# A two-layer graph kernel on one core: upper slot layers cut to a tile's last nodes, and a start-up written out in order

## The chip, the core and the metric

One core of one Trainium2 chip runs the whole program. The metric is device time in microseconds, from launch to end. The engines are PE (matmul, with its weight loads shown as PEld), DVE (vector), ACT (scalar), POOL (GpSimd, which also issues the indirect transfers) and SP (which only issues transfers). DMA transfers are issued by SP, ACT and POOL and are carried out by the core's 16 DMA engines.

## The reference, cut to what matters

There are 4096 nodes with 128 features each and a 0/1 adjacency matrix of 4096 x 4096 with about 32 neighbours a node. Two layers follow each other.

```python
# layer 0: graph attention, 8 heads
Wh = einsum('nd,hde->hne', nodes, W)
e = leaky_relu(f1[:, :, None] + f2[:, None, :], 0.2)      # f1 = Wh.a1, f2 = Wh.a2
att = softmax(where(adj > 0, e, -9e15), axis=-1)
h = elu(einsum('hnm,hmd->hnd', att, Wh))
x = layernorm(nodes + elu(concat_heads(h) @ W1 + b1)) * gamma + beta
# layer 1: neighbours, less every m-th one, sorted per feature; three quantiles
keep = mask & ~((rank + 1) % skip == 0)
svals = sort(where(keep, x, big), axis=1)
agg = mean of svals at ceil(q * n_keep) - 1, q in (0.25, 0.5, 0.75)
out = (0.5 * agg + 0.5 * x) @ W.T + b + x
```

## The kernel before, in words

The kernel works with lists of neighbours instead of the matrix. It has these stages.

**Search.** `neighbours` reads 128 rows of adj in two halves of 1 MB (`adj_t`, issued by ACT), turns each into signs on ACT (`sgn`, which also counts), and lets PE add, in PSUM tiles `key` of 512 columns, the sign times 8192 and a falling number of the column (`parts`, filled by POOL; `markb` and `oneb` are the fixed operands). DVE takes the eight largest of every 128 columns (`first`, L592) and then, in eight rounds, the largest 64 of those (L597 and L599). A tile of 128 nodes is eight such pieces; the selection runs one tile behind. `complete_records` works out, per group of up to four tiles, which neighbours layer 1 drops.

**Blocks.** The 32 tiles are taken in three blocks of 4, 9 and 19 (`BLOCKS`). Inside a block `rank_by_count` sorts the nodes by their number of neighbours (`ranks`), and POOL scatters their records (`rec`, list, own number, features, f1, f2) to DRAM in that order, so that each tile of a block then holds nodes of like count. `CAPS` gives the most neighbours that a node of each sorted tile may have.

**Attention for a tile.** `read_lists` loads the 128 records (`R`, four loads by SP) and spreads the lists into layers: a layer `(s0, w)` covers the list places from s0 to s0 + w of all 128 nodes with w gathers, each of which serves P // w nodes (`k`) completely. A layer narrower than 32 needs its own four loads by SP (`narrow`) and its own small DVE operations; there is one `narrow` buffer for each width. `fetch_rows` issues one indirect gather (L194, POOL) for each slot, 128 rows of 544 bytes from `xt_d` (features and f2) into tiles `G` of 16 slots, of which there are six. `attend` adds f1 (`z`), applies the exponential, sums it per node on PE (`den`, own) and hands the sum back (`rz`, ownT), with P // w // 4 matmuls for each layer in each of the two; it then spreads the weights (`wide`, L932) and multiplies every slot's rows on PE (`y`, L944). The dense part and the layer norm follow, and POOL scatters the 128 finished rows to `x1_d`.

**Order.** In the blocks the order on DVE, PE, ACT and POOL is the order of the code (`manual_schedule`). Each `step` issues the gathers of one tile, attends the tile before it, prepares the lists two tiles ahead and mixes in a share of the search of the next block. In the last tile of a block, the rest of the search and `rank_by_count` come first on DVE, and the scatters of the next block's records are mixed into that tile's gathers on POOL, one after every two, beginning when so few gathers are left that they just suffice:

```python
if among and left % 2 == 0 and left <= 2 * len(among) + 4:
    scatter(nc, *among.pop(0))
```

The next block's first lists can be loaded only after the last of these scatters has landed.

**Start.** Before the first block the constants (`own`, `ownT` and others) are made, the search of block 0 runs (L317), and `node_rows` loads W, x, a1 and a2, forms `wa`, transposes the 32 tiles of x on PE one at a time, multiplies them by `wa` to get f1 and f2 (`F`) and stores features and f2 to `xt_d`. Here the framework's scheduler chooses the order on the engines; x, W and a1, a2 are loaded by SP.

**Layer 1.** After the 32 tiles, 1024 gathers fetch the rows of `x1_d`, and DVE runs a sorting network cut to what the quantiles need (L1155). If any count exceeds its bound (`bad`, summed into `total`), a general path behind L501 computes everything again.

Of the kernel before, what the change touches and what calls it, by code (L numbers as in the profile page):

```python
# [9 lines left out]
F32 = mybir.dt.float32  # L10
# [44 lines left out]

TURNS = {4: range(4), 9: range(9), 19: [0, 1, 2, 3, 18, 4, 5, 6, 7, *range(9, 18), 8]}
# [33 lines left out]
def layers(c):  # L90


    out = []
    s = 0
    for w in (32, 32, 16, 8, 4):
        if (c + 3) // 4 * 4 - s >= w:
            out.append((s, w))
            s += w
    return out

# [117 lines left out]
def kernel(  # L218
# [33 lines left out]
    iota(nc, pidx, [[0, 1]], cm=1)  # L252
    jp1 = const.tile([P, L], F32, name="jp1")
    iota(nc, jp1, [[1, L]], base=1)

    own = {}
    for w in (32, 16, 8, 4):
        k = P // w
        v = const.tile([P, k], F32, name=f"v{w}")
        iota(nc, v, [[-w, k]], cm=1)  # L260
        own[w] = const.tile([P, k], F32, name=f"own{w}")
        nc.vector.tensor_scalar(own[w], v, 0.0, None, ALU.is_ge)
        nc.vector.scalar_tensor_tensor(own[w], v, float(w), own[w], ALU.is_lt, ALU.mult)


    ownT = {}
    for w in (32, 16, 8, 4):
        k = P // w // 4
        v = const.tile([4, k, P], F32, name=f"vT{w}")
        iota(nc, v, [[-4 * w, k], [1, P]], cm=-w)  # L270
        ownT[w] = const.tile([4, k, P], F32, name=f"ownT{w}")
        nc.vector.tensor_scalar(ownT[w], v, 0.0, None, ALU.is_ge)
        nc.vector.scalar_tensor_tensor(ownT[w], v, float(w), ownT[w], ALU.is_lt, ALU.mult)

# [3 lines left out]
    nc.sync.dma_start(W_sb, W.rearrange("h d e -> d h e"))  # L278
# [4 lines left out]
    consts = dict(  # L283
        W_sb=W_sb, W1_sb=W1_sb, vecs=vecs, eps_t=eps_t, ident=ident, own=own, ownT=ownT
    )
# [11 lines left out]
    nc.gpsimd.iota(  # L297
        rec.bitcast(I32)[:, :, R_OWN], pattern=[[P, NT]], base=0, channel_multiplier=1
    )
    parts = adjp.tile([64, N], BF16, name="parts", bufs=1)  # L300
    markb = adjp.tile([P, P], BF16, name="markb", bufs=1)
    nc.vector.memset(oneb, 1.0)
    nc.vector.tensor_scalar(markb, ident, MARK, None, ALU.mult)

    nc.gpsimd.memset(parts, 0.0)
    iota(nc, parts[0:1, :], [[-64, N // 64], [0, 64]], base=N)
    iota(nc, parts[32:33, :], [[0, N // 64], [-1, 64]])
    rowi = adjp.tile([P, P], F32, name="rowi", bufs=1)
    iota(nc, rowi, [[1, P]])
    nc.vector.tensor_scalar(before, rowi, pidx, None, ALU.is_gt)  # L310
# [6 lines left out]
    for _ in search(0, BLOCKS[0]):  # L317
        pass
    with tc.tile_pool(name="setup", bufs=1) as sp, tc.tile_pool(
        name="setup_ps", bufs=2, space=PSUM  # L320
    ) as pp:
        node_rows(tc, sp, pp, rec, x, W_sb, a1, a2, Wl, wa, WlT, ident, bad, xt_d)
# [3 lines left out]
        for i, big in enumerate((-BIG, BIG)):  # L326
            fill = sp.tile([P, D], F32, name=f"fill{i}")
            nc.vector.memset(fill, big)
            nc.sync.dma_start(x1_d[N + i * P : N + (i + 1) * P, :], fill)
# [6 lines left out]
    weigh, store, tail = [], [], []  # L336
    consts["small"] = pp.tile([P, 512], F32, name="small")
# [6 lines left out]

    def prepare(b, i, t0):
        n = BLOCKS[b]
        i = TURNS[n][i]
        return read_lists(tc, attp, recs_d[b], i, CAPS[n][i], t0 + i, bad, narrow)
# [49 lines left out]
    with tc.manual_schedule(engines=ORDERED):  # L398
        ranks = rank_by_count(tc, cp, kp, num, jp1, before, oneb, 0, BLOCKS[0])
        for v in store_records(0, 0, ranks):  # L400
            scatter(nc, *v)
        for b, n in enumerate(BLOCKS):
# [103 lines left out]
def node_rows(tc, sp, pp, rec, x, W_sb, a1, a2, Wl, wa, WlT, ident, bad, xt_d):  # L506

    nc = tc.nc
    c = NT // 4
    for i in range(4):  # L510
        nc.sync.dma_start(
# [3 lines left out]
    a_b = sp.tile([P, 2, H * D], F32, name="a_b")  # L515
    for i, a in enumerate((a1, a2)):
        nc.sync.dma_start(a_b[:, i, :], a.rearrange("h d -> (h d)").partition_broadcast(P))
    wl_sb = sp.tile([P, D], F32, name="wl_sb")
    nc.scalar.dma_start(wl_sb, Wl)
    wl_ps = pp.tile([P, D], F32, name="xt_ps")  # L520
    nc.tensor.transpose(wl_ps, wl_sb, ident)
    nc.scalar.copy(WlT, wl_ps)
    for i in range(2):
# [4 lines left out]
        nc.vector.tensor_reduce(wa[:, ts(i, H)], wprod, AX.X, ALU.add)  # L528
    F = sp.tile([P, NT, 2 * H], F32, name="F")
    for t in range(NT):  # L530
        xt_ps = pp.tile([P, P], F32, name="xt_ps")
        nc.tensor.transpose(xt_ps, rec[:, t, R_X : R_X + D], ident)
        xT = sp.tile([P, P], F32, name="xT", bufs=2)
        nc.scalar.copy(xT, xt_ps)
        f_ps = pp.tile([P, 2 * H], F32, name="f_ps")
        nc.tensor.matmul(f_ps, lhsT=xT, rhs=wa, start=True, stop=True)
        nc.scalar.copy(F[:, t, :], f_ps)
    for dst, src in ((R_F1, F[:, :, 0:H]), (R_X + D, F[:, :, H:])):
        nc.vector.tensor_scalar(rec[:, :, dst : dst + H], src, FMAX, -FMAX, ALU.min, ALU.max)
    sq = sp.tile([P, NT, 2 * H], F32, name="sq")  # L540
# [6 lines left out]
    for i in range(4):  # L547
        nc.sync.dma_start(
            xt_d[ts(i, c * P), :].rearrange("(t p) w -> p t w", p=P),
            rec[:, ts(i, c), R_X:],  # L550
        )
    pad = sp.tile([P, XW], F32, name="pad")
    nc.vector.memset(pad[:, 0:D], 0.0)
    nc.vector.memset(pad[:, D:], PADF)
# [873 lines left out]
```

## Time and profile before

| what | value |
|---|---|
| median of 3 runs | 4632.38 us (4607.63 to 4632.42) |
| profiled execution, its own time | 3702.95 us |
| its span | 3701.2 us |
| PE, DVE, ACT, POOL busy | 1228.3, 2746.5, 403.4, 2421.0 us |
| gathers of `G` (L194) | 1180, 1174.8 us busy, mean 996 ns, 478.8 us idle before them |
| gathers of `vals` (layer 1) | 1024, 1052.1 us busy |
| mean granted TensorE clock | 0.581 |

The profile is of one execution, which was shorter than the timed runs. Busy time is what an engine's instructions took; the idle time of a group is what its engine waited just before the group's instructions, with the releaser that ended most of it. A line such as L194 is that of a helper and gathers all its callers; the tile names tell them apart.

### The profile page before, as it was taken

What the parts mean: (1) busy time and instruction counts of PE and PEld (TensorE: products, weight loads), DVE (VectorE), ACT (ScalarE), POOL (GpSimd) and SP (SyncE); (2) the same over time, 40 slices, a digit from 0 to 9 for tenths busy, and PEclk for the clock granted to TensorE, in tenths of its full rate; (3) what the DMA queues carried; (4) which work ended last, traced back from release to release, by engine and by line L of the source; (5) the groups of instructions that cost most, each with busy time, mean ns of one, the idle gap of its engine ahead of it and who ended that gap; (6) DMA issues with size and microseconds to landing.
All of it is one profiled execution on the core that took longest, in us unless ns stands there. A gap on an engine that the chain in (4) does not pass through costs nothing. (4 is left out here: it accounts for less than half of the span.)

```text
span 3701.2 us, 23191 instructions
## 1 busy us (share of the span) xinstructions
PE 1228.3 (33%) x5433; PEld 936.3 (25%) x5433; DVE 2746.5 (74%) x7565; ACT 403.4 (11%) x603; POOL 2421.0 (65%) x2388
## 2 busy tenths in 40 slices
PE   6483767773673544454450000000000000000011
PEld 2043544453562443444440000000000000000011
DVE  8774688782541222127637999999999999999998
ACT  3121222220120111111110000000000000000000
POOL 1657674467777777777747777677657565667630
PEclk9975676655575555565555555555555555555555
DMA  6432544322222221222211111111111111111100
GB/s 211 156 99 67 182 137 136 128 72 62 59 54 55 53 55 52 53 66 57 55 33 49 47 47 46 43 46 46 37 38 48 36 42 40 44 44 49 42 19 3
DMA packets 110291, 241.33 MB, mean 65 GB/s; under 512 B 46976, under 2 KB 63360, under 8 KB 101952
## 3 DMA queue, kind: packets, MB, share of 16 engines
q0 software_dynamic: 76160, 160.24, 15.5%
q10 hardware_dynamic: 9360, 67.18, 5.2%
q1 hardware_dynamic: 24624, 12.34, 1.4%
q8 instruction: 45, 0.74, 0.1%
q14 instruction: 102, 0.84, 0.1%
HBM read 228.44 MB, written 11.15 MB: 65 GB/s over the span
## 5 line engine op out<-in xcount | busy, mean ns | idle before, releaser
L194 POOL DMA_INDIRECT G<-xt_d,idx x1180 | 1174.8, 996 | 478.8 <-issue 336.4
L194 POOL DMA_INDIRECT vals<-x_d,idx x1024 | 1052.1, 1027 | 337.6 <-issue 298.5
L1155 DVE TENSOR_TENSOR work<-work 128x512 f32<-128x512 f32 (+6 forms) x1405 | 961.0, 714 | 0.4
L1174 PE MATMUL st_ps<-dg,goal 128*128 128x128 f32 x286 | 71.2, 426 | 1645.3 <-DVE goal L1155 1574.9
L1155 DVE TENSOR_TENSOR work<-work,work 128x512 f32<-128x512 f32 (+5 forms) x958 | 606.4, 658 | 0.7
L1174 PEld LDWEIGHTS st_ps<-dg,goal 128*128 128x128 f32 x286 | 63.2, 322 | 1651.7 <-issue 1650.8
L944 PE MATMUL y<-wide,G 128*128 128x32 f32 (+3 forms) x2360 | 460.3, 371 | 23.9 <-DVE wide L932 23.9
L944 PEld LDWEIGHTS y<-wide,G 128*128 128x128 f32 x2360 | 440.2, 286 | 47.5 <-DVE wide L932 26.3
L887 DVE TENSOR_TENSOR z<-G,f1x 128x128 f32<-128x128 f32 (+2 forms) x92 | 29.9, 335 | 471.5 <-DMA G<-xt_d,idx 467.3
L592 DVE MAX8 first<-key 128x8 f32<-128x128 f32 x1024 | 227.8, 282 | 108.4 <-PE key L628 108.3
L203 POOL DMA_INDIRECT out_dram<-o,own_i x32 | 45.6, 1425 | 297.4 <-ACT o L1200 277.8
L625 PE MATMUL key<-sgn,markb 128*128 128x512 bf16 x256 | 141.6, 554 | 162.3 <-DVE first L592 108.9
L1126 DVE COPY junk<-still 128x1 f32<-128x1 f32 x1295 | 194.7, 150 | 0.0
L901 PE MATMUL small<-z,own 128*4 128x32 f32 (+3 forms) x436 | 50.2, 284 | 380.6 <-ACT z L894 380.6
L1155 DVE TENSOR_TENSOR work<-vals 128x1024 f32<-128x1024 f32 (+8 forms) x140 | 138.8, 1009 | 46.4 <-DMA vals<-x_d,idx 46.1
L586 ACT ACTIVATE sgn<-adj_t 128x2048 bf16<-128x2048 int32 x64 | 122.0, 1907 | 340.7 <-PE key L625 304.5
L1173 ACT ACTIVATE dg<-ident,wt 128x128 f32<-128x128 f32 x143 | 47.5, 394 | 957.2 <-PE st_ps L1174 956.8
L916 PE MATMUL rz<-rden,ownT 4*128 4x32 f32 (+3 forms) x436 | 104.7, 411 | 117.3 <-DVE rden L912 96.0
L628 PE MATMUL key<-parts,oneb 64*128 64x512 bf16 x256 | 140.4, 549 | 6.3 <-POOL parts L212 6.3
L974 PE MATMUL small<-W_sb,late 128*128 128x128 f32 x512 | 118.7, 425 | 33.5 <-DVE late L971 33.5
L901 PEld LDWEIGHTS small<-z,own 128*4 128x4 f32 x436 | 27.1, 102 | 398.1 <-ACT z L894 385.8
L916 PEld LDWEIGHTS rz<-rden,ownT 4*128 4x128 f32 x436 | 91.9, 302 | 133.5 <-DVE rden L912 68.4
(179 smaller groups left out, 1891.7 us busy)
## 6 DMA issues: line engine op xcount, KB each, us to landing
adj_t<-in_adj_dram ACTq DMA_DIRECT2D x64, 1024.0 KB
G<-xt_d,idx POOLq DMA_INDIRECT x1180
vals<-x_d,idx POOLq DMA_INDIRECT x1024
R<-rec_d SPq DMA_DIRECT2D x128, 26.2 KB
xt_d<-rec SPq DMA_DIRECT2D x4, 544.0 KB
rec<-in_x_dram SPq DMA_DIRECT2D x4, 512.0 KB
W_sb<-in_L_gnn_W_dram SPq DMA_DIRECT2D x2, 512.0 KB
a_b<-in_L_gnn_a_dram SPq DMA_DIRECT2D x2, 512.0 KB
```

Of the source, the lines that this page charges most:

```text
L194: nc.gpsimd.indirect_dma_start(out=dst, out_offset=None, in_=rows, in_offset=bass.IndirectOffsetOnAxis(ap=idx, axis=0),)
L586: nc.scalar.activation(sgn, adj_t, AF.Sign, accum_out=cnt[:, i : i + 1])
L592: nc.vector.max(first[:, ts(c0 // CW + c, 8)], key[:, ts(c, CW)])
L625: nc.tensor.matmul(key, lhsT=markb, rhs=sgn[:, ts(b, 512)], start=True, stop=False)
L628: nc.tensor.matmul(key, lhsT=oneb[0:64, :], rhs=parts[:, ts(r, 512)], start=False, stop=True)
L901: nc.tensor.matmul(den[0:4, :].rearrange("p (g r h) -> p r g h", r=k // 4, h=H)[:, r], lhsT=own[w][:, ts(r, 4)], rhs=z[:, layer[i] : layer ...
L916: nc.tensor.matmul(rz[:, layer[i] * H : (layer[i] + w) * H], lhsT=ownT[w][:, r, :], rhs=rden.rearrange("p (g r h) -> p r g h", r=k // 4, h ...
L944: nc.tensor.matmul(yf[:, ts(g, c)], lhsT=G[:, col + g - g0, 0:D], rhs=pf[:, ts(g, c)], start=(i == 0 and g % (w // 2) == w // 2 - 1), stop ...
L974: nc.tensor.matmul(o, lhsT=hv[:, h, :], rhs=consts["W1_sb"][:, h, :], start=(h == 0), stop=(h == H - 1))
L1126: nc.vector.tensor_copy(junk, late["still"])
L1155: nc.vector.tensor_tensor(slots_of(dst, (j, c, s, m), size), slots_of(a, (i, c, s, m), size), slots_of(b, (i + d, c, s, m), size), op,)
L1174: nc.tensor.matmul(st_ps[:, u, :], lhsT=goal[:, (j * k + u) * D : (j * k + u + 1) * D], rhs=dg, start=(j == 0), stop=False,)
```

## The change

The change has two parts. First, a layer may begin at a node group other than the first: `(s0, w, g0)` leaves out the gathers below g0, so that only the last nodes of the sorted tile get these places. `LAYERS` lists such layers for eleven tiles; elsewhere the layers are as before. The bound on the counts then rises along the tile (`steps_of`, `nodeq`).

```diff
+LAYERS = {
+    (4, 1): [(0, 32, 0), (32, 8, 7)],
+    (4, 2): [(0, 32, 0), (32, 4, 0), (36, 8, 7)],
+    (4, 3): [(0, 32, 0), (32, 16, 0), (48, 16, 15)],
+    (9, 0): [(0, 16, 0), (16, 8, 0), (24, 4, 2)],
+    (9, 4): [(0, 32, 0), (32, 4, 1)],
+    (9, 6): [(0, 32, 0), (32, 4, 0), (36, 4, 2)],
+    (9, 8): [(0, 32, 0), (32, 16, 0), (48, 16, 14)],
+    (19, 1): [(0, 16, 0), (16, 8, 0), (24, 4, 1)],
+    (19, 9): [(0, 32, 0), (32, 4, 2)],
+    (19, 17): [(0, 32, 0), (32, 8, 0), (40, 4, 1)],
+    (19, 18): [(0, 32, 0), (32, 16, 0), (48, 16, 13)],
+}
+def steps_of(parts):
+    held = [0] * P
+    for s0, w, g0 in parts:
+        for q in range(g0 * P // w, P):
+            if held[q] == s0:
+                held[q] += w
+    return held[0], [(q, held[q] - held[q - 1]) for q in range(1, P) if held[q] > held[q - 1]]
...
 def read_lists(...)
-    nc.vector.tensor_scalar(bad[:, 4, t : t + 1], R[:, R_NUM : R_NUM + 1], float(cap), None, ALU.is_gt)
+    cap, rises = min(cap, steps_of(layer_list)[0]), steps_of(layer_list)[1]
+    over = R[:, R_NUM : R_NUM + 1]
+    for q, more in rises:
+        up = ap.tile([P, 1], F32, name="up", bufs=3)
+        nc.vector.tensor_scalar(up, nodeq, float(q), -float(more), ALU.is_ge, ALU.mult)
+        nc.vector.tensor_tensor(up, up, over, ALU.add)
+        over = up
+    nc.vector.tensor_scalar(bad[:, 4, t : t + 1], over, float(cap), None, ALU.is_gt)
...
 def fetch_rows(...)
-        for g in range(w):
+        for g in range(g0, w):
...
 def attend(...)      # z, den, rz, wide and y work on w - g0 slots of a layer
-                rhs=z[:, layer[i] : layer[i] + w, :],
+                rhs=z[:, layer[i] : layer[i] + w - g0, :],
...
-        spread = [P, w, k, H]
+        spread = [P, n, k, H]          # n = w - g0
```

Second, everything up to the first gather is put under `manual_schedule`. The number rows are split in two tiles of 512 and 3584 columns, cleared on DVE; `own` and `ownT` are made after the scatters of block 0; the loads of W, a1, a2, Wl and x are issued by ACT; and `node_rows` becomes a generator that is advanced once after each search piece of block 0, with rows of x transposed four tiles at a time.

```diff
-    nc.gpsimd.memset(parts, 0.0)
-    iota(nc, parts[0:1, :], [[-64, N // 64], [0, 64]], base=N)
-    iota(nc, parts[32:33, :], [[0, N // 64], [-1, 64]])
-    for _ in search(0, BLOCKS[0]):
-        pass
...
+    ) as pp, tc.manual_schedule(engines=ORDERED):
+        for v in parts:
+            nc.vector.memset(v, 0.0)
+        nc.vector.memset(oneb, 1.0)
+        for v, base in zip(parts, (N, N - N // 8)):
+            n = v.shape[1] // 64
+            iota(nc, v[0:1, :], [[-64, n], [0, 64]], base=base)
+            iota(nc, v[32:33, :], [[0, n], [-1, 64]])
+        nc.vector.tensor_scalar(markb, ident, MARK, None, ALU.mult)
+        iota(nc, pidx, [[0, 1]], cm=1)
...
+        rows = node_rows(tc, sp, pp, rec, x, W, W_sb, a1, a2, Wl, wa, WlT, ident, bad, xt_d)
+        for i, _ in enumerate(search(0, BLOCKS[0])):
+            if i > 0:
+                next(rows, None)
+        for _ in rows:
+            pass
+        nc.vector.tensor_scalar(before, rowi, pidx, None, ALU.is_gt)
...
         for v in store_records(0, 0, ranks):
             scatter(nc, *v)
+        own = {}            # own and ownT, as they were, now here
...
 def node_rows(...)
+    load = nc.scalar.dma_start
+    load(W_sb, W.rearrange("h d e -> d h e"))
+    yield
+    for i, a in enumerate((a1, a2)):
+        load(a_b[:, i, :], a.rearrange("h d -> (h d)").partition_broadcast(P))
+    load(wl_sb, Wl)
+    yield
     for i in range(4):
-        nc.sync.dma_start(
+        for _ in range(3):
+            yield
+        load(
             rec[:, ts(i, c), R_X : R_X + D],
             x[ts(i, c * P), :].rearrange("(t p) d -> p t d", p=P),
         )
...
-    for t in range(NT):
-        xt_ps = pp.tile([P, P], F32, name="xt_ps")
-        nc.tensor.transpose(xt_ps, rec[:, t, R_X : R_X + D], ident)
-        xT = sp.tile([P, P], F32, name="xT", bufs=2)
-        nc.scalar.copy(xT, xt_ps)
-        f_ps = pp.tile([P, 2 * H], F32, name="f_ps")
-        nc.tensor.matmul(f_ps, lhsT=xT, rhs=wa, start=True, stop=True)
-        nc.scalar.copy(F[:, t, :], f_ps)
+    for t in range(0, NT + 8, 4):
+        if f_ps is not None:
+            nc.scalar.copy(F[:, t - 8 : t - 4, :], f_ps)
+            f_ps = None
+        if xT is not None:
+            f_ps = pp.tile([P, 4, 2 * H], F32, name="f_ps")
+            for u in range(4):
+                nc.tensor.matmul(f_ps[:, u, :], lhsT=xT[:, ts(u, P)], rhs=wa, start=True, stop=True)
+            xT = None
+        yield
+        if t < NT:
+            xt_ps = pp.tile([P, 4 * P], F32, name="xt_ps")
+            for u in range(4):
+                nc.tensor.transpose(xt_ps[:, ts(u, P)], rec[:, t + u, R_X : R_X + D], ident)
+            xT = sp.tile([P, 4 * P], F32, name="xT", bufs=2)
+            nc.scalar.copy(xT, xt_ps)
+        yield
```

## The prediction

> **What bounds the kernel now.** I read the page first: one core, span 3701.2 us, DVE 74% busy, POOL 65%, no engine full. The chain view is of no use here (it names only the last 32 us), so I went to busy time by stage, then to the timelines of POOL and DVE at the seams between stages.
>
> ```profile
> 270.00:358.00 88.00, 43.29 (x189) 35.22 (x189) 42.09 (x146) 9.59 (x9) 67.13 (x67) 0.56 0.21 58
> 358.00:843.00 485.00, 345.26 (x1429) 221.82 (x1429) 384.21 (x1468) 127.14 (x132) 300.00 (x305) 0.64 0.41 129
> 843.00:1884.00 1041.00, 522.79 (x2694) 479.19 (x2693) 369.34 (x1114) 129.22 (x142) 795.15 (x790) 0.58 0.22 56
> ...
> 1924.00:3701.00 1777.00, 125.56 (x542) 107.35 (x542) 1723.82 (x3944) 57.33 (x180) 1130.83 (x1087) 0.52 0.14 40
> ```
> Columns: stretch, its length, busy PE, PEld, DVE, ACT, POOL with instruction counts, clock, DMA share, GB/s. From 270 to 358 and from 843 to 1884 POOL sets the pace (DVE busy 48% and 35%); from 358 to 843 DVE does (79%, the rest waits for PE); after 1924 the sort is DVE's (97%). The seams, from the timelines (start, duration, instruction, idle before it and its releaser):
>
> ```profile
> 26.15 1.68 DVE L592 MAX8 first<-key 128x8 f32<-128x128 f32 x8
> ...
> 98.33 1.12 POOL L203 DMA_INDIRECT rec_d<-rec,ranks  x1 [72.42 <-DVE ranks L768]
> ...
> 113.05 0.97 POOL L194 DMA_INDIRECT G<-xt_d,idx  x1 [5.56 <-DVE f1b L833]
> 114.32 0.95 POOL L194 DMA_INDIRECT G<-xt_d,idx  x1 [0.31 <-issue]
> ...
> 139.73 0.14 DVE L642 TENSOR_TENSOR num<-cnt 128x1 f32<-128x1 f32 x1
> ...
> 152.35 0.14 DVE L642 TENSOR_TENSOR num<-cnt 128x1 f32<-128x1 f32 x1
> ...
> 270.49 0.94 POOL L194 DMA_INDIRECT G<-xt_d,idx  x1 [21.71 <-PE y L944]
> ...
> 307.51 0.15 DVE L768 CAST ranks<-rank 128x1 int32<-128x1 f32 x1
> ...
> 321.16 1.00 POOL L203 DMA_INDIRECT rec_d<-rec,ranks  x1 [0.30 <-DVE v L996]
> ...
> 357.85 0.15 DVE L805 TENSOR_SCALAR bad<-R 128x1 f32<-128x1 f32 x1 [32.31 <-DMA R<-rec_d]
> ...
> 843.31 1.00 POOL L203 DMA_INDIRECT rec_d<-rec,ranks  x1 [0.39 <-DVE ranks L768]
> ```
> To be seen: (1) DVE's search begins only at 26 us and everything up to the first scatter at 98.33 waits for its ranks. (2) A gather costs 1.25 us where POOL is free (113.05 to 114.32, and a median of 1.25 in block 2). (3) A search tile in written order takes 12.6 us (139.73 to 152.35). (4) At 321 the scatters wait not for ranks (ready 307.5) but for the 38 gathers of the last tile that stand before them on POOL; DVE then waits 32 us for R. (5) At 843 the scatters come 0.4 us after the ranks.
>
> **Part 1, the start.** Removed from ahead of the search on DVE: the constants own and ownT, which waited for POOL's fills, and wprod/wa, which waited for a_b:
>
> ```profile
> 2.32 5.21 DVE L272 TENSOR_SCALAR ownT<-vT 4x128 f32<-4x128 f32 x1
> ...
> 6.12 1.91 ACT L586 ACTIVATE sgn<-adj_t 128x2048 bf16<-128x2048 int32 x1 [2.67 <-DMA adj_t<-in_adj_dram]
> ...
> 21.17 1.23 DVE L525 TENSOR_TENSOR wprod<-W_sb,a_b 128x1024 f32<-128x1024 f32 x1 [3.16 <-DMA a_b<-in_L_gnn_a_dram]
> ```
> The first sgn is ready at 8.0 in any case. In the new order PE needs only the small part of the number rows (two fills of 512 elements, about 0.5 us each by the row of 3.85 us for 4096) and the search waits on DVE for pidx (used by nodeq), which stands behind the large fills on POOL: two of 3584 at 3.4 us each, so about 9.7. Sum on DVE from 9.7: tile 0 has no selection yet and goes at PE's pace, 8.4 us (the same stretch before: 119.84 to 128.26); three tiles of 12.6 = 37.8; the selection alone of the last tile, 8 x 0.82 = 6.6; wprod and wa 4.9 (two pairs of 1.23 + 1.21); rec and sq from F 2.4; the records and ranks, some 53 small operations, 10 (7.3 of it stands from 90.7 to 98.0 before, some 3 stood among the selections from 81.9); hand-offs 0. Ranks at 79.8; with 0.5 to POOL and 0.5 of hand-offs the first scatter stands at **80.8** instead of 98.3: 17.5 earlier.
>
> Can data keep up? ACT now issues every load in order with its compute: eight for adj, W_sb, two a_b, wl and four of x. In the order of issue, the load of wl waits for the fourth adj load, and sgn of tile 1 stands behind it. By the bytes (slices of before: 4.1 MB landed at 13 us, 6 at 19.5, 8 at 26) the fourth adj lands near 15, sgn follows at 17.3, PE wants it at 17: no more than 1 us. x takes 3.3 us of issue each (four in 13.1 us on SP before); a tile leaves ACT over 8 of its 12.6 us, so they fit. PE's first transposes (tile 2, about 38 us) have x by then. Transposes in fours: 32 xT copies of 0.27 become 8, and F's 32 copies become 8; ACT is not the bound, I count nothing. The stores to xt_d start near 69 instead of 87.5 and need about 10 us, before a first gather at 97: covered; if the cover went, the first gather would wait for them.
>
> Here the Trainium skill speaks against it: "DMA: Bandwidth & Descriptors" (Issuing engines are not separate DMA queues) says that loads moved to another engine run on the same 16 DMA engines and only issue time is saved. By that alone part 1 would gain nothing if bytes were the limit: 8 MB of adj and 4.3 MB of the rest. The row decides: a tile of 2 MB per 12.6 us asks 166 GB/s, the trace moved 8 MB in the first 26 us (308 GB/s). What helps is the order, not the queue.
>
> Added behind the scatters: 8 iotas on POOL (2.5 us by their rows) and 16 operations on DVE, then the lists of tile 0. POOL and DVE are idle there (107.5 to 112.1 wait for R). "SBUF — State Buffer" (Who interferes with whom) says a DVE operation in a two-port mode and a GpSimd operation exclude each other for a whole instruction; the trace agrees at L272 above (0.1 us of work, 5.2 taken). By the rule none of it overlaps: 2.5 + 4 us after the last scatter, first gather 2 us late; by the row, at most one iota (1.0 us) is waited for. I take 1.5, ends 0 and 3. First gather at **97**: **16 earlier**. Ends for part 1: 5 and 22.
>
> **Part 2, fewer gathers.** Slots fall from 1180 to 1127: block 0 168 to 151, block 1 336 to 317, block 2 676 to 659. Where each counts:
>
> Block 0. Tile 3 starts its gathers when y of tile 1 frees G (270.49), a matter of DVE and PE. The DVE chain is shifted by 16, less 2 (one more list with four SP loads in tile 2), plus 2 (tile 1's upper layer needs 4 own/ownT matmuls less in each sum and one y of 128 columns for four of 256): ranks at 291.5. POOL now needs 60 -> 49 slots, so 27 gathers, not 38, before the first scatter: 254 + 35 = 289. The scatters start at **291.5** instead of 321.2: 29.7 earlier, of which 13.7 come from here. Then ranks end the wait.
>
> Block 1 is DVE's; its 19 gathers fall into POOL's idle time and save nothing by themselves. At its end 8 instead of 22 gathers precede the scatters, but ranks are the later: nothing. Changed on DVE and PE: tile 3's sums go from 15 matmuls to 5 each (minus 10 x 0.25 and 10 x 0.4), two wide copies are gone (2 us), and some y: about -8. Tile 6 of block 1 gets three layers: +12 in each sum (+7.6), a wide of 512, a list: +2. Tile 8: two lists of 16 wide share one buffer, so the second loads only after DVE has read the first: 3.3 us from issue to use (R, 354.56 to 357.85), and 2.4 of list work; tile 6 waits likewise. Ends: -10 if PE's part is hidden, +12 if all is on the path. I take **+3**, since DVE idles 21% there for PE.
>
> Block 2 is POOL's without a gap over 2 us: 17 x 1.25 = **21 us** saved. Its lists are prepared two tiles ahead; beside idle DVE. G: tile 18 takes four buffers before and after, so the look-ahead stays. The drain (1884 to 1924) and the sort are unchanged.
>
> Sum: 16 + 13.7 - 3 + 21 = **48**, on the profiled execution's 3702.95: 3655, or 1.3%.
>
> The three timed runs have a median of 4632.4, 929 us above the profiled one, and no view shows where. If it lies in the untouched sort, 48 us is saved: 4584. If it is spread evenly, 1.3%: 4572. I take the middle: **4577**.
>
> **Rivals.**
> - *The start does not move.* ACT's in-order issues or the bytes hold the search. For: 13.1 us for four x on SP. Against: the byte sum. Loses 16: 4632 - 32 = 4600. Chance 0.22.
> - *Gathers cost more unprofiled.* The 929 us over some 2,300 indirect transfers is 0.4 each (estimate); then POOL is the bound in block 1 too and all 53 count: 53 x 1.65 = 87, and 16: 4529. For: POOL's share; against: the sort has half of them. Chance 0.16.
> - *Block 1 eats it.* Its extra lists and sums at the +12 end, and a few more from PE at clock 0.6: 4610. Chance 0.06.
> - *Slower: the ACT queue starves the search.* Every DMA on ACT waits for one several places earlier before sgn may go on. Price: x 13 us, and up to eight waits of a 1 MB landing (4 us at 262 GB/s): 45. It decides once the first gather comes after 113 + 32 = 145, against 97 forecast; at all of it, with PE blocked behind late x, 4640 or more. Chance 0.06.
> - *It does not do what it says.* A node with more neighbours than its slots would send the kernel into the general path at L501, many times longer. The counts of these inputs fit (largest in the tile of 60: 50, in a place with 64), so no chance.
>
> **Numbers.** Forecast 0.50, of which 0.44 lies beyond 1% (below 4586; 1% is about what a measurement of this kernel tells from no change). Faster 0.44 + 0.16 = 0.60; same 0.06 + 0.22 + 0.06 = 0.34; slower 0.06. Range: from just inside the 4529 case, 4535, to 4622.
>
> **What would show it.** First MAX8 at 9 to 11; first scatter at 78 to 84, first gather 94 to 100, with xt_d not its releaser; second set of scatters near 291, released by DVE ranks, not by POOL's own queue; third near 816; last gather of block 2 near 1831; sort unchanged in length. I am wrong if ACT shows long waits on DMA before sgn of tiles 1 to 3, if POOL shows new idle time on y in block 2, or if the sort's length moves.

## The result, and the profile after

| | median, us | runs | against before |
|---|---|---|---|
| before | 4615.10 (4579.41 to 4658.33) | 20 | |
| after | 4584.24 (4538.39 to 4628.19) | 20 | 0.9912, 95% interval 0.9885 to 0.9939 |

The ratio leaves out runs that are more than 1.5% above the fastest of their kernel; by the medians of all 20 it is 0.9933. So the changed kernel is 0.7 to 0.9% faster, 31 to 41 us. The forecast was 4577 us, the range 4535 to 4622; it was made from a median of 4632.38, so the saving forecast was 55 us. Two later comparisons of the same pair gave 0.9895 (0.9863 to 0.9926) and 0.9949 (0.9922 to 0.9975): 48 and 23 us. So the direction stands and the size lies between 23 and 48 us.

The profile of before that the prediction rests on (3702.95 us) is of an execution a fifth shorter than every timed run above, while the profile after (4612.32 us) is of the usual length. So the two can't be laid side by side; a second profile of before (experiment 1, 4572.22 us) can be laid beside the profile after.

The lines that answer to those shown of before stand in the timelines of VectorE and POOL after (start, duration, instruction, idle before it and what ended that):

```profile
10.42 1.68 DVE L650 MAX8 first<-key 128x8 f32<-128x128 f32 x8
...
24.21 0.89 DVE L650 MAX8 first<-key 128x8 f32<-128x128 f32 x4 [4.34 <-PE key L686]
...
95.86 1.12 POOL L230 DMA_INDIRECT rec_d<-rec,ranks  x1 [54.61 <-issue]
...
112.40 0.97 POOL L221 DMA_INDIRECT G<-xt_d,idx  x1 [4.98 <-issue]
...
401.91 0.98 POOL L230 DMA_INDIRECT rec_d<-rec,ranks  x1 [10.17 <-DVE rk L817]
...
1147.75 0.98 POOL L230 DMA_INDIRECT rec_d<-rec,ranks  x1 [20.40 <-DVE ranks L826]
...
2453.83 0.94 POOL L221 DMA_INDIRECT G<-xt_d,idx  x1 [0.30 <-issue]
```

The search begins at 10.42 instead of 26, as forecast, yet the first scatter comes at 95.86, not at 80.8, and the first gather at 112.40, not at 97. The second set of scatters is released by DVE and no longer by POOL's own queue, as forecast; but that shows little here, since in the second profile of before DVE releases it too (429.22, after 12.21 us for `rk`). Everything after the first gather is later than in the first profile of before, in untouched code too.

Busy time by stage after (length, then busy PE, PEld, DVE, ACT, POOL with counts, clock, DMA share, GB/s): block 1, block 2, sort.

```profile
402.00:1148.00 746.00, 402.06 (x1549) 259.55 (x1551) 397.18 (x1513) 133.51 (x139) 305.28 (x315) 0.56 0.28 85
1148.00:2454.00 1306.00, 498.36 (x2503) 464.00 (x2504) 343.03 (x1049) 123.83 (x134) 752.25 (x771) 0.55 0.17 44
2539.00:4610.00 2071.00, 124.82 (x542) 107.54 (x542) 1736.60 (x3944) 58.85 (x185) 1162.29 (x1088) 0.51 0.12 35
```

In block 2 no engine is busy for more than 58% of the stage, POOL included, where POOL was at 76% in the first profile of before (795 of 1041 us). The costliest group of the page and the group of `rden` (busy, mean ns, idle before and what ended most of it) name the new waits:

```profile
L221 POOL DMA_INDIRECT G<-xt_d,idx x1127 | 1090.3, 967 | 1109.5 <-PE y L1012 696.0
...
L976 DVE TENSOR_SCALAR rden<-small 4x256 f32<-4x256 f32 x32 | 13.0, 407 | 648.1 <-remote 583.6
```

POOL waits 696 us for y to free G buffers (100 in the first profile of before), and DVE waits 584 us ahead of `rden`, for a signal whose sender the trace doesn't place ("remote"). A gather itself costs what it did: 0.97 us and 0.30 to the next.

The prediction named three signs of being wrong, and the profile after shows all three: ACT waits 9.77 us on DMA before its third `sgn`, POOL waits for y in block 2, and the sort takes 2071 us instead of 1777. The second and third are not the change's doing, since the second profile of before has them too (601 us and 2051 us, experiment 1); the first cost the start some 4 us.

### The profile page after: what moved, and what is told of

It reads as the page before. It is cut to its first block, busy times and chain, and to the rows that moved or that the text cites. A ratio compares the mean times of both kernels' runs of the same rounds, so it can differ in the third digit from the quotient of the medians.

```text
span 4610.5 us, 23017 instructions
## 1 busy us (share of the span) xinstructions
PE 1260.0 (27%) x5372; PEld 961.7 (21%) x5375; DVE 2754.3 (60%) x7608; ACT 399.4 (9%) x555; POOL 2364.5 (51%) x2344
## 5 line engine op out<-in xcount | busy, mean ns | idle before, releaser
L221 POOL DMA_INDIRECT G<-xt_d,idx x1127 | 1090.3, 967 | 1109.5 <-PE y L1012 696.0
L221 POOL DMA_INDIRECT vals<-x_d,idx x1024 | 1076.9, 1052 | 337.5 <-issue 302.0
L1012 PE MATMUL y<-wide,G 128*128 128x32 f32 (+2 forms) x2254 | 463.1, 381 | 97.3 <-issue 71.6
L976 DVE TENSOR_SCALAR rden<-small 4x256 f32<-4x256 f32 x32 | 13.0, 407 | 648.1 <-remote 583.6
L982 PE MATMUL rz<-rden,ownT 4*128 4x32 f32 (+6 forms) x460 | 113.3, 416 | 515.9 <-DVE rden L977 431.4
L982 PEld LDWEIGHTS rz<-rden,ownT 4*128 4x128 f32 x460 | 101.8, 317 | 532.2 <-issue 364.0
L1031 PE MATMUL hT<-late,W_sb 128*128 128x128 f32 x512 | 112.8, 409 | 238.1 <-issue 160.2
L1223 DVE TENSOR_TENSOR work<-vals 128x1024 f32<-128x1024 f32 (+8 forms) x140 | 138.7, 1007 | 32.7 <-DMA vals<-x_d,idx 32.4
L1031 PEld LDWEIGHTS hT<-late,W_sb 128*128 128x128 f32 x512 | 104.7, 312 | 249.7 <-issue 167.1
```

The lines of the kernel that those rows point to most:

```text
L221: nc.gpsimd.indirect_dma_start(out=dst, out_offset=None, in_=rows, in_offset=bass.IndirectOffsetOnAxis(ap=idx, axis=0),)
L982: nc.tensor.matmul(rz[:, layer[i] * H : (layer[i] + w - g0) * H], lhsT=ownT[w][:, r, :], rhs=rden.rearrange("p (g r h) -> p r g h", r=k // ...
L1012: nc.tensor.matmul(yf[:, ts(g, c)], lhsT=G[:, col + j - a, 0:D], rhs=pf[:, ts(j, c)], start=(i == 0 and g % (w // 2) == w // 2 - 1), stop= ...
L1031: nc.tensor.matmul(hT[:, ts(h, P)], lhsT=consts["W_sb"][:, h, :], rhs=yT[:, h, :], start=True, stop=True)
L1223: nc.vector.tensor_tensor(slots_of(dst, (j, c, s, m), size), slots_of(a, (i, c, s, m), size), slots_of(b, (i + d, c, s, m), size), op,)
```

## Experiments

Ratios are to the kernel before, run on the same chip beside them. Experiments 1 to 4 ran on one chip, 5 to 8 on a second, 9 and 10 on a third, 11 and 12 on a fourth; the chip of the first comparison is not on record. Each profile is of one execution.

**1. The kernel before, profiled again** (no edit).

> The kernel before, profiled once more. Theory A (the change made the attention stages slower than the first profile of before shows: POOL waits 696 us for y in the profile after, 100 us in the profile before): this profile is near 3703 us again and block 2 takes about 1040 us. Theory B (the first profile of before is of a rare quick execution; timed executions of both kernels run as the profile of after does): span near 4615 us, block 2 (second scatters to last G gather) over 1300 us instead of 1041, POOL waits for y 600 us or more, the sort near 2080 us instead of 1777. First scatter at 98 and first gather at 113 in both, since no gathers run there.

Measured: 4572.22 us, span 4570.5. First scatter 99.6, first gather 114.8, scatters 429.2 and 1153.2, last G gather 2434.3, sort from 2519.1. Its busy time by stage (block 1, block 2, sort) and its costliest group:

```profile
429.00:1153.00 724.00, 390.20 (x1546) 254.17 (x1547) 396.60 (x1493) 133.76 (x139) 324.89 (x333) 0.58 0.31 90
1153.00:2434.00 1281.00, 513.99 (x2542) 477.94 (x2542) 340.52 (x1032) 123.97 (x134) 774.54 (x787) 0.56 0.20 46
2519.00:4570.00 2051.00, 125.64 (x542) 107.90 (x542) 1736.77 (x3944) 58.81 (x185) 1162.79 (x1088) 0.51 0.14 35
```

```profile
L194 POOL DMA_INDIRECT G<-xt_d,idx x1180 | 1150.9, 975 | 1035.7 <-PE y L944 601.0
```

Theory B holds in the main: this is the profile after, with the old code. Block 2 takes 1281 us (over 1300 was expected), POOL waits 601 us for y, the sort takes 2051 (near 2080 was expected). That the short execution is a rare one turned out otherwise (experiments 9 to 12). The busy times hardly differ from the first profile of before (DVE 1737 us in the sort against 1724); what has grown is idle time. The 870 us between the two profiles, and so most of the 929 between the first profile and the timed runs, are stalls in all attention blocks and in the sort.

**2 and 3. The two halves, and 4. the whole beside them.** Start alone: `LAYERS = {}`. Layers alone: the kernel before with `LAYERS`, `steps_of` and the edits in `read_lists`, `fetch_rows` and `attend`.

> The new start with the old lists (1180 gathers). My sum: 16 us less than before, of which the profile of after shows so far only 98.3 to 95.9 at the first scatter and 113.0 to 112.4 at the first gather. Rival (the start does not move): 0 to 2 us less, and the whole of the measured 31 to 41 us belongs to the layers.

> The old start with the new lists (1127 gathers). My sum: 13.7 - 3 + 21 = 32 us less than before. Rival (POOL's gathers and the work of PE and DVE exclude each other in the timed executions, so that each of the 53 gathers counts wherever it stands): 53 x 1.25 = 66 us less. Rival (the layers' extra lists and matmuls eat the saving): 10 us less or none, and then the start would have to carry it.

> The changed kernel, beside its two halves on the same chip. If the halves add up: start_only and layers_only together give its saving, 31 to 41 us by the 20 runs. If they overlap (an earlier start only makes POOL wait longer for y): it saves no more than the larger half.

| kernel | median, us | ratio, 95% interval |
|---|---|---|
| start alone | 4595.25 | 1.0004, 0.9973 to 1.0034 |
| layers alone | 4572.70 | 0.9946, 0.9920 to 0.9973 |
| both | 4546.96 | 0.9895, 0.9863 to 0.9926 |

(before: 4593.18.) The start saves nothing that can be measured; the layers carry the gain, 25 us here against the 32 expected. The halves add up to 23 us and the whole shows 48; the intervals of sum and whole reach 19 and 14 us to each side (the former an estimate from those of the halves) and overlap, so no interplay is shown.

**5. Why the start did not move.** Fewer of the transposed rows stand among the search's matmuls, and the ranks come ahead of the copies of F (cut to the lines that do it):

```
...
-            if i > 0:
-                next(rows, None)
+            if 0 < i < 25:
+                next(rows)
+                done += 1
+        for _ in range(36 - done):
+            next(rows)
+        ranks = rank_by_count(...)
         for _ in rows:
             pass
...
```

> As the changed kernel, but only four of the eight groups of transposed rows of x stand among the search's matmuls, the other four behind its last one, and the ranks are worked out ahead of the copies of F to the records. Theory A (in the new start PE is the bound from 40 to 76 us: 27.5 of 30 us busy, DVE waiting 0.3 to 1.1 us for key in each group): the last search tile takes some 15 instead of 19 us, the first scatter moves from 95.9 to about 84 to 87 and the first gather from 112.5 to about 101; the time falls by some 10 us against the changed kernel. Theory B (the loads on ACT's queue hold the search): tile 1 still begins at 24 and everything behind it stays, first scatter within 2 us of 95.9.

Busy time by stretch, first the profile after (tiles 2 and 3 of the search), then the second profile of before in the same part of its search:

```profile
40.00:70.00 30.00, 27.52 (x91) 15.93 (x91) 22.95 (x95) 9.78 (x17) 0.83 (x3) 1.00 0.34 114
```

```profile
50.00:74.00 24.00, 24.00 (x76) 11.74 (x75) 18.65 (x88) 12.05 (x39) 0.00 (x0) 1.00 0.40 133
```

PE is busy for 27.5 of 30 us, and for all of 24 us in the kernel before: in this stretch the search is PE's. DVE's timeline of after (experiment 4) shows the pace of tile 3, the last search tile, from the last group of tile 2 to its own last group:

```profile
55.27 0.89 DVE L650 MAX8 first<-key 128x8 f32<-128x128 f32 x4 [0.62 <-PE key L686]
...
74.45 0.89 DVE L650 MAX8 first<-key 128x8 f32<-128x128 f32 x4 [0.63 <-PE key L686]
```

That is 19.2 us a tile instead of 12.6. With four of the eight groups of rows moved behind the search, the same tile takes 14.0 us (54.50 to 68.50) and the ranks come at 89.6. POOL's timeline of this kernel:

```profile
90.98 1.12 POOL L230 DMA_INDIRECT rec_d<-rec,ranks  x1 [79.76 <-DVE sq L608]
...
96.33 0.97 POOL L230 DMA_INDIRECT rec_d<-rec,ranks  x1 [3.39 <-DMA rec_d<-rec,ranks]
...
111.45 0.98 POOL L221 DMA_INDIRECT G<-xt_d,idx  x1 [4.98 <-issue]
```

The first scatter moves from 95.9 to 91.0, less than the 84 to 87 of theory A, because the rank work on DVE took 13.3 us and the copies of F stood behind it. The first gather moves from 112.6 to 111.4 only: the four scatters, 2.8 us apart in after, now stand 5.3, 4.1 and 2.7 us apart. The store of xt_d is issued at 90.1 there, beside them, and at 81.4 in after; that it slows them is likely, and was not tried by itself. The time is 4592.82, ratio 0.9953 (0.9925 to 0.9982): no better than the three ratios of after. PE as the bound of this stretch of the search is shown; a gain from relieving it is not.

**6. Block 1 with its old lists**: the four `(9, ...)` entries of `LAYERS` are left out.

> As the changed kernel, but the tiles of block 1 keep their old lists (336 gathers there instead of 317). My sum put block 1 at 3 us of loss. Theory A (its three-list tile 6 and two lists of 16 in tile 8 cost more than that: block 1 took 742 and 746 us in two profiles of after, 724 in one of before): 15 to 20 us less than the changed kernel. Theory B (the difference is scatter between executions; a gather saved counts): 0 to 24 us more than the changed kernel (19 x 1.25).

Measured 4584.86, ratio 0.9936 (0.9915 to 0.9957): inside the span of the three results for after, so neither theory is confirmed. In its profile block 1 is shorter (714 us; 741 to 746 in three profiles of after). The profiles place this: up to the sums of tile 2 of block 1 (`rden`; tiles are counted from 0) it runs as the kernel after does, and from there to the ranks at the end of the block it takes 427 us instead of 458. First this kernel, then after:

```profile
688.69 0.40 DVE L972 TENSOR_SCALAR rden<-small 4x256 f32<-4x256 f32 x1
...
1116.10 0.17 DVE L822 CAST ranks<-rank 128x8 int32<-128x8 f32 x1
```

```profile
689.76 0.40 DVE L976 TENSOR_SCALAR rden<-small 4x256 f32<-4x256 f32 x1
...
1147.30 0.17 DVE L826 CAST ranks<-rank 128x8 int32<-128x8 f32 x1
```

So the new lists lengthen block 1; the timed total does not show it, and its interval is 10 us wide to each side.

**7 and 8. Breaks in POOL's trains of gathers.** The stalls first, on the timeline of after (all engines, block 2):

```profile
1897.39 1.28 PE L966 MATMUL small<-z,own 128*4 128x256 f32 x18
...
1930.90 0.94 POOL L221 DMA_INDIRECT G<-xt_d,idx  x1 [0.30 <-issue]
1932.15 0.98 POOL L230 DMA_INDIRECT x_d<-x_t,mine  x1 [0.30 <-issue]
1939.58 0.41 DVE L976 TENSOR_SCALAR rden<-small 4x256 f32<-4x256 f32 x1 [55.93 <-remote]
...
1957.00 0.97 POOL L221 DMA_INDIRECT G<-xt_d,idx  x1 [23.88 <-PE y L1012]
```

PE's sums for this tile are recorded as done by 1898.7 (ends of matmuls are modelled), the semaphore (the signal between engines) that they raise changes at 1939.55, and DVE starts on it at once. Between lie 41 us in which POOL issues gathers 1.25 us apart and almost nothing else runs. The release comes 6 us after the train has ended. In four tiles in a row the trains ended at 1933.1, 2006.9, 2078.5 and 2152.4, and DVE went on at 1939.6, 2013.4, 2084.0 and 2159.2. Then PE makes y, G comes free, and the next train begins. Gathers (some 50 us) and computing (some 23) thus take turns, 73 us a tile, where they overlapped in the first profile of before.

One kernel fills the second G buffer of each tile three times before it gathers into it, the other waits for the sixteenth gather to land:

```
                 G, col = ap.tile([P, 16, XW], F32, name="G", bufs=6), 0
+                opened += 1
+                if opened == 2:
+                    for _ in range(3):
+                        nc.gpsimd.memset(G, 0.0)
```
```
             if col == 16:
+                if G is not None:
+                    nc.gpsimd.tensor_copy(ap.tile([P, 1], F32, name="seen", bufs=1), G[:, 15, 0:1])
                 G, col = ap.tile([P, 16, XW], F32, name="G", bufs=6), 0
```

> As the changed kernel, but POOL stops gathering for some 6 us in the middle of each tile (three fills of the second G buffer, about 2 us each, before it is gathered into). Theory A (while POOL issues gathers back to back, finished work of PE and DVE is held up until the train of gathers ends; a break lets it go): POOL's wait for y, 696 us in the profile after, falls by more than the 200 us that the fills cost, and the time falls by 100 us or more. Theory B (what is held goes only when POOL is quiet, not merely doing something else): up to 200 us slower. Theory C (gathers have nothing to do with the stalls): no change, since POOL waits for y about 20 us a tile anyway.

> As the changed kernel, but after every 16 gathers POOL waits until the last of them has landed (it copies one element of it) before it issues the next. Some 45 such waits of 2 to 3 us. Theory A (a break in the train lets the held work of PE and DVE go): faster by 100 us or more, POOL's wait for y shrinks. Theory B (a break so short does nothing): 0 to 130 us slower.

| kernel | median, us | ratio, 95% interval |
|---|---|---|
| fills | 4401.90 | 0.9539, 0.9488 to 0.9589 |
| waits | 4415.46 | 0.9570, 0.9491 to 0.9649 |

(before: 4620.47.) POOL does more, and the kernels are 4.6 and 4.3% faster than before, where the change alone gives 0.5 to 1.1% in three sets on other chips. POOL's wait for y falls from 604 to 696 us, in three profiles of after, to these rows of the table of waits (total, times, longest), with fills and with waits:

```profile
POOL G L221 <- PE y L1016: 270.2, 12, 47.6
```

```profile
POOL G L221 <- PE y L1014: 337.1, 20, 49.2
```

With the waits, 52 breaks stand POOL still for 95.3 us in all. (With the fills, 32.7 us more stand ahead of the fills themselves.) Theory A holds for both: an unbroken train of gathers holds up the others, and a break of 2 us lets much of it go. What in the chip is held was not found out, nor whether the sums themselves or only their signal come late.

**9 to 12. Breaks in the sort as well**, on the changed kernel and on the kernel before, and the changed kernel once more. Beside the waits of experiment 8:

```
                     gather(nc, vals[:, a : a + D], x1_d, idx[:, t, j : j + 1])
+                    if (j * k + u) % 16 == 15:
+                        nc.gpsimd.tensor_copy(sp.tile([P, 1], F32, name="seen", bufs=1), vals[:, a : a + 1])
```

> The changed kernel with a break after every 16 gathers (POOL waits for the last to land) in the attention blocks and in the sort as well. In the attention blocks alone the break was worth 4.3%. Theory A (in the sort too, back-to-back gathers hold up DVE: the sort takes 2043 to 2071 us in five profiles, with DVE busy 1740, and 1778 in the first profile of before): the sort falls to 1800 to 1900 us, the whole to 4150 to 4250. Theory B (the sort's length has another cause): 4390 to 4420, as with the breaks in the attention blocks alone, or up to 120 us above that where the 64 new waits of 1.8 us count.

> The kernel before with the same breaks, beside the changed kernel with them. Theory A (with the held work let go, the sum of the prediction applies, as in the first profile of before: 2 for the start as measured, 13.7 for block 0, 21 for block 2, 3 lost in block 1): 30 to 40 us above the changed kernel with breaks. Theory B (the gathers count only where they hold other engines up; breaks take that away): within 15 us of it. Theory C (POOL is then the bound everywhere and each of the 53 gathers and the 3 breaks fewer count): 65 to 75 us above it.

> The changed kernel once more, beside the kernel before. The chip decides which case is seen: the kernel before takes 4593 to 4620 us on two of the chips used so far and 3714 on the third. If this one is of the fast kind, gathers and compute overlap as in the first profile of before, and the sum applies with the start as measured (2 instead of 16): 13.7 + 21 - 3 + 2 = 34 us less than before, 3680; and as the breaks cost the kernel before 89 us there and the changed kernel lies 65.6 above before with them, a saving of 23 to 34. If it is of the slow kind: 30 to 50 us less, as in the first two comparisons.

> The changed kernel with breaks after every 16 gathers in the attention blocks and the sort, once more. On a chip of the fast kind it cost 1.7% against before. On one of the slow kind, Theory A (back-to-back gathers hold up DVE in the sort too): 4150 to 4300; Theory B (the sort's length there has another cause): 4390 to 4450, as with the breaks in the attention blocks alone.

| chip | kernel | median, us | ratio, 95% interval |
|---|---|---|---|
| third | before | 3713.61 | |
| third | before, with breaks | 3802.69 | 1.0236, 1.0218 to 1.0254 |
| third | after, with breaks | 3779.20 | 1.0166, 1.0144 to 1.0189 |
| fourth | before | 4598.78 | |
| fourth | after | 4565.93 | 0.9949, 0.9922 to 0.9975 |
| fourth | after, with breaks | 4094.12 | 0.8929, 0.8880 to 0.8979 |

On the third chip the unchanged kernel took 3714 us in the median of 11 runs (3707 to 3723), as long as the first profile of before. Below, "fast chip" means this one and "slow chips" the others, as they were in these runs. On the fast chip the breaks cost the kernel before 2.4%, so that the first theories, made for a slow one, do not apply. On the fourth chip they take 10.3% off the changed kernel (4565.93 to 4094.12), more than theory A expected. The changed kernel without breaks saved 23 to 33 us there, where 30 to 50 were expected. The sort on the fourth chip with breaks:

```profile
2320.00:4110.00 1790.00, 125.37 (x542) 107.12 (x542) 1723.62 (x3944) 58.66 (x185) 1217.83 (x1144) 0.52 0.15 40
```

1790 us, against 2043 to 2095 in the profiles of slow chips without breaks in the sort, and 1785 to 1791 with breaks on the fast chip: theory A, all of the sort's excess came from the trains. VectorE's busy tenths in 40 slices, in the profile after and with breaks on the fourth chip:

```profile
DVE  6274446655142212212254289989987977887788
```

```profile
DVE  6367446766424302212254379999999999999998
```

The right half is the sort: 7 and 8 become 9. The fast chip also lets the change be read with gathers and compute overlapping. Busy time from the first gather to the third set of scatters, and in block 2, before with breaks and after with breaks:

```profile
114.00:858.00 744.00, 504.95 (x1924) 308.94 (x1924) 561.32 (x2169) 174.29 (x180) 475.81 (x500) 0.67 0.40 120
858.00:1969.00 1111.00, 527.15 (x2681) 483.91 (x2681) 365.25 (x1106) 128.53 (x140) 802.80 (x820) 0.56 0.23 53
```

```profile
112.00:855.00 743.00, 509.84 (x1897) 309.14 (x1898) 558.88 (x2186) 174.33 (x180) 437.01 (x464) 0.66 0.39 117
855.00:1942.00 1087.00, 520.99 (x2652) 479.92 (x2651) 368.64 (x1128) 128.32 (x140) 784.25 (x803) 0.56 0.23 53
```

Blocks 0 and 1 together take 744 and 743 us; block 2 takes 24 us less. The timed difference of the two is 3802.69 - 3779.20 = 23.5 us, between theory A of experiment 10 (30 to 40) and theory B (within 15).

## Why the prediction was right, and where it was not

The time came out near for partly wrong reasons, and so in part by luck: on the chip where the sum can be laid beside its terms, half of it is there. By its steps, from the profiles of the fast chip (with breaks on both sides), where gathers and compute overlap as in the profile that it was made on:

| step | forecast | measured |
|---|---|---|
| start, to the first gather | -16 | -2.4 (114.0 to 111.6) |
| block 0, beyond the shift | -13.7 | -19.2 (210.9 to 191.7) |
| block 1 | +3 | +18.2 (533.2 to 551.4) |
| block 2 | -21 | -23.5 (1110.8 to 1087.3) |
| drain and sort | 0 | +1.9 |
| sum | -48 | -25 |

**The start** failed at "the search goes at 12.6 us a tile, hand-offs 0". The 12.6 was taken from a search tile of block 1 that has no transposes beside it. The transposes in fours were costed on ACT alone ("ACT is not the bound, I count nothing"); on PE a group of four is 1.11 + 1.89 us, and eight groups are 24 us among some 35 us of key matmuls. Tile 3 cost 6.6 us more for it, and tile 2 some 3. Tile 1 lost another 4: ACT stood from 11.1 to 16.6 before its fifth load of adj, issued four more loads until 21.0, and only then made sgn (forecast 17.3), so that DVE waited 4.34 us. In the trace's signals that fifth load reuses the semaphore of the 64 KB load of beta into vecs, issued on SP at 2.3 and landed at 16.55. The byte sum had ACT's own loads in view and not SP's small one under the same semaphore. The last selection and the rank work took a little longer than forecast. The first MAX8 (10.42) and the 1.5 us between scatter and gather (16.7 against 15.2) were right, and xt_d was not the releaser. So the rival "the start does not move" is what happened, by another cause than either that it named: PE's sum of work is the same in both kernels (59.8 and 59.5 us up to the first gather).

**Block 0** moved as forecast, and for the reason given: on the fast chip the second scatters came 19 us after the ranks in before and come 0.8 us after them now. DVE's wait for R behind the scatters shrank from 38.39 to 14.91 us, here on the two timelines of the fast chip:

```profile
362.21 0.15 DVE L807 TENSOR_SCALAR bad<-R 128x1 f32<-128x1 f32 x1 [38.39 <-DMA R<-rec_d]
```

```profile
344.17 0.16 DVE L871 TENSOR_TENSOR up<-up,R 128x1 f32<-128x1 f32 x1 [14.91 <-DMA R<-rec_d]
```

**Block 1** is the second step that failed: "I take +3", with ends of -10 and +12, and it measured +18. The 20 us won by the start and block 0 were still there at the sums of tile 3 of block 1, and gone at the ranks that end it, before with breaks and after with breaks on the fast chip:

```profile
579.15 0.41 DVE L915 TENSOR_SCALAR rden<-small 4x256 f32<-4x256 f32 x1
...
855.24 0.17 DVE L770 CAST ranks<-rank 128x8 int32<-128x8 f32 x1
```

```profile
558.72 0.41 DVE L980 TENSOR_SCALAR rden<-small 4x256 f32<-4x256 f32 x1
...
854.32 0.17 DVE L828 CAST ranks<-rank 128x8 int32<-128x8 f32 x1
```

Between them the changed tiles 4 and 6 are summed and the lists of 6 and 8 are prepared; this stretch grows from 276.1 to 295.6 us. At its end POOL, out of gathers, stands 20.39 us for the ranks, where it stood 0.30. On slow chips the same stretch takes 355 to 364 us in three profiles of kernels with the old lists in block 1 and 372 to 379 in five with the new ones, the kernel of experiment 6 among the former. So it is the lists of block 1 that cost the time. The prediction had the mechanism and mis-sized it: a second list in the same `narrow` buffer is loaded only after DVE has read the first. For tile 6 and then for tile 8, prepared two tiles ahead, DVE waits (3.3 us had been taken for each):

```profile
608.78 0.18 DVE L892 COPY ids<-narrow 128x32 int32<-128x32 int32 x1 [2.44 <-DMA narrow<-rec_d]
...
730.71 0.18 DVE L892 COPY ids<-narrow 128x32 int32<-128x32 int32 x1 [6.11 <-DMA narrow<-rec_d]
```

Before had no such wait there. DVE's wait for the search's keys grew as well, in the same stretch (total, times, longest):

```profile
DVE first L594 <- PE key L630: 38.0, 21, 3.4
```

```profile
DVE first L652 <- PE key L688: 45.4, 22, 7.5
```

PE, with the extra sums, is busy 213.5 instead of 205.4 us there, at a granted clock of 0.59 instead of 0.61; DVE's own work is the same (232.7 and 231.7). The two waits make 16 of the 19.5 us. So the low rival "block 1 eats it" (chance 0.06) is what happened to blocks 0 and 1 on the fast chip: together -10.7 was forecast and -1 measured. On the slow chips the two blocks take 1038 us in the second profile of before and 1035, 1046 and 1039 in three of after; with the old lists of block 1 (experiment 6) 1005, in one profile.

**Block 2** was right where POOL sets the pace: 17 gathers of 1.25 are 21, and 23.5 was measured. On the slow chips it takes 1281 us before, and 1263, 1278 and 1306 after: POOL waits 600 us and more for y there, so fewer gathers need not shorten it.

**The way to the timed median** failed as a step: "no view shows where" was answered by taking the middle of two guesses. It was the chip (or the hour, which the runs don't part from it): the sort, untouched, holds some 270 to 300 us of the difference and the blocks the rest. The rival "gathers cost more unprofiled" had the right suspect and the wrong mechanism: the gather's own time is unchanged, and it holds others up. On the slow chips 23 to 48 us are saved, by the layers as far as experiment 3 shows, and no profile places them: single executions of one kernel differ by more (4562 to 4664 us for before in one set).

The port rule weighed in part 1 ("SBUF — State Buffer", Who interferes with whom, of the Trainium skill) doesn't cover the stalls. By it only the port pair shared by DVE and GpSimd causes contention, for one instruction at a time; here the signal of PE's sums comes 41 us late, across some 27 gathers. The measurement decides. In part 1 the trace agrees with the rule in kind: the operation on ownT that took 5.21 us beside POOL's fills takes 0.87 us after, though not the 0.1 us that the prediction took for its bare work.

## What to carry to other kernels

Before work is moved earlier on one engine, add up what every engine has to do in the stretch: here the row of PE, 24.00 busy in 24.00 us, said that an earlier start on DVE would not shorten that part of the search while the transposes stand in it. A list that saves gathers where POOL has time to spare still costs its own loads: here two lists in one buffer were waits of 2.4 and 6.1 us on the busiest engine. Such a list belongs where gathers set the pace. Where profile and timed runs differ by a fifth, profile again until one fits the timed runs before any edit is costed; and where POOL gathers back to back while others stand still, try a wait for every sixteenth gather, on each chip that matters.

## What the hardware showed unasked

- The same kernel takes 4593 to 4620 us on three chips and 3714 on a fourth, with nearly the same busy times (in the sort DVE is busy 1737 and 1724 us, in the second and the first profile of before) and a gather of about 1.25 us in both. Each chip was seen in one set of runs, so that chip and hour can't be told apart.
- On the slow chips, work of PE and DVE goes on late while POOL issues indirect gathers without a break. A wait after every 16 took 472 us off the changed kernel there (4565.93 to 4094.12) and all of the excess off the sort, but only part of it off block 2 (1263 us without breaks and 1174 with them on the fourth chip; 1087 on the fast one).
- On the fast chip the same breaks cost the kernel before 89 us. Breaks pay on the slow chips alone. The changed kernel without breaks was not timed on the fast chip, so that its gain there, 23.5 us with breaks on both sides, is open.
